# Row means removed inside the turning matrix of a GRU stage: a four-layer graph network on one Trainium2 core

## Chip, core and metric

One NeuronCore of a Trainium2 chip runs the whole program. The metric is the device time of one execution in microseconds (us). Three timed runs of the kernel before gave 720.81, 721.02 and 722.56, median 721.02. A further execution was taken with the hardware profiler; it took 719.45, and its span, from the first to the last recorded instruction, is 717.7.

## What is computed

3327 nodes with 64 features each, an adjacency matrix of zeros and ones, and four layers, each of the form x = x + layer(relu(layernorm(x))):

- 0: attention in hyperbolic space (curvature 1), a sum over neighbours weighted by a sigmoid and an arctangent-like distance;
- 1: a decay sum over neighbours, times a weight matrix, plus a bias;
- 2: a signed graph attention with two GRU cells;
- 3: the hyperbolic attention again, with a learned curvature r.

The parts that matter here:

```python
def _layernorm(x, axis=-1, eps=1e-5):
    m = jnp.mean(x, axis=axis, keepdims=True)
    v = jnp.var(x, axis=axis, keepdims=True)
    return (x - m) / jnp.sqrt(v + eps)
...
def gru_cell(x, h, w_ih, w_hh, b_ih, b_hh):
    ...
    return (1.0 - z) * n + z * h
```

A layer's output is multiplied by the diagonal of the adjacency matrix (dcol below) where the masks of the fast path ask for it, and added to x; then the next layer takes the row mean, the row variance, and the relu of what is normed.

## The kernel before, in words

The nodes are padded to 26 tiles of 128 rows. X holds all of x in SBUF as 128 partitions x 26 tiles x 64 features; tiles 0 to 12 and 13 to 25 are the two halves ("HALVES", "(h t)" in X2). One program does the four layers one after the other; each is planned by hand: inside tc.manual_schedule the instructions of an engine run in the order in which they are written, and an instruction that waits holds up those behind it on its engine.

**Layer 2, plain_gat (L1841).** The attention sums run block by block on PE (block, L1865, matmuls L1871), into four PSUM tiles, one for each group of columns in COLS: group 0 has 4 tiles of each half, groups 1, 2 and 3 have 3. A dictionary `todo` (L1944) hangs small work of the other engines behind certain blocks: `inverse` behind block 12 (degree maximum L1934 on DVE, then a relu, logarithm and exponential on ACT), `inverse2` behind block 17 (L1941, L1942 on DVE). Then two GRU cells run over the four groups, eight steps in a software pipeline: gate matmuls (products, L1987 and L1992), sigmoids (L2000) and tanh (L2011) on ACT, state on DVE (L2007 to L2027).

**Turning back.** The GRU output lies with features on the partitions. turn_back(k) (L2032) brings group k back to rows: for every tile of the group PE multiplies up to four terms, one after the other into the same PSUM place, by the identity (L2043; group 3 has a single term and uses a transpose, L2041). Group k takes PSUM bank 4 + k; two neighbouring banks make one "slot", and waits are kept by slot, so that groups 0 and 1 share one and groups 2 and 3 another. scale(k) multiplies by the diagonal, on ACT tile by tile with the diagonal's column as the scale (L2059), for group 3 on DVE (L2054); use(k) adds the product to X on DVE (L2063). The end of plain_gat:

```python
tanh(K - 1)
scale(0)
turn_back(1)
scale(1)
turn_back(2)
state(K - 1)
use(0)
turn_back(3)
use(1)
scale(2)
...
```

**Layer 3, hyperbolic_series (L350).** It opens with the layer norm: the row mean by halves (L449, L450), X minus mean into H (L452), squares on ACT (L453), relu and its square on ACT (L455, L456), the row sums of both squares (L458, L466, L469), and between them the inverse root by bit tricks (root_by_bits, L125: eight dependent DVE steps on 128x26 values). L472 multiplies the norms' squares by the inverse variance. From there a chain of 26-wide DVE steps leads to Xr, the normed and scaled features (L481), their fp16 parts hi and lo (L482, L484), the transposes on PE (L542, L517), the attention vectors (L560 to L578) and the main loop (L877). POOL meanwhile builds extra columns from x2 (L493 to L506) and, before that, zeroes X0 (L436) and sets constants in Xe (L437, L439). The "late" tiles of the adjacency matrix, loaded by SP (L1447), are only counted for zeros (L1459) during the main loop.

The main loop runs four column chunks by 26 blocks: sigmoid (ACT, L629), mask (POOL, L632), distance matmuls (PE, L643, L644), arctangent (ACT, L649), weights (DVE, L654), sums (PE, L664, L672). After it come the sums' way back and about seventy 26-wide steps (factors, L721) that end in the factors ah and am (L858, L860).

**The tail (L912 to L930).** X becomes X + ah Xr + am M. DVE does Xr (L916, L919). ACT multiplies the first 22 tiles of M by am, one instruction a tile with am's column as its scale (L923); DVE does the last four ("own") and adds M in three pieces, each stored at once by SP (L2104).

hyperbolic_series serves layer 0 too, where x arrives by DMA.

Of the kernel before, what the change touches and what calls it, by code (L numbers as in the profile page):

```python
# [49 lines left out]
def tile_gnn4(ctx: ExitStack, tc: tile.TileContext, x, adjT, att0, b0, w1, bias1, w_gat, a_gat,  # L50
# [296 lines left out]
            after.append(of_r)  # L347
        return wlr, bcol, cc, sqc, isqc, um2, maxn2

    def hyperbolic_series(r, params, ok, masks=None, done=None, ahead=None, then=None, checks=None):  # L350

# [10 lines left out]


        KE = D + 9
        left_row = rows[0 if r is None else 1]
        W = 512
        with ExitStack() as st:
# [60 lines left out]
            with room(name="hsp", bufs=1) as tp, room(name="hsps", bufs=2, space=PSUM) as ps, \  # L430
                    tc.manual_schedule(engines={mybir.EngineType.Activation, mybir.EngineType.DVE,
                                                mybir.EngineType.PE, mybir.EngineType.Pool}):
                H, R, sq, sr = [tp.tile([P, T, D], F32, name=n) for n in ("H", "R", "sq", "sr")]
                Xe = tp.tile([P, T, KE + 9], F16, name="Xe")
                E, Fe = Xe[:, :, D:KE], Xe[:, :, KE:]
                G.memset(X0, 0.0)  # L436
                G.memset(E[:, :, 6:], SX)  # L437
                for k, part in enumerate(f16_parts((1.0 - PB / PA) * SX)):
                    G.memset(Fe[:, :, 6 + k:7 + k], part)  # L439
# [4 lines left out]
                    return tp.tile([P, T], F32, name=name)  # L444


                mean, v, rv, ax, ia2 = [new(n) for n in ("mean", "v", "rv", "ax", "ia2")]
                for ts in HALVES:
                    V.reduce_sum(mean[:, ts], X[:, ts, :], axis=AX.X)  # L449
                V.tensor_scalar(mean, mean, 1.0 / D, None, op0=OP.mult)  # L450
                for ts in HALVES:
                    V.tensor_sub(H[:, ts, :], X[:, ts, :], wide(mean[:, ts]))  # L452
                    A.activation(sq[:, ts, :], H[:, ts, :], AF.Square)  # L453
                for ts in HALVES:
                    A.activation(R[:, ts, :], H[:, ts, :], AF.Relu)  # L455
                    A.activation(sr[:, ts, :], R[:, ts, :], AF.Square)  # L456
                for ts in HALVES:
                    V.reduce_sum(v[:, ts], sq[:, ts, :], axis=AX.X)  # L458
                V.tensor_scalar(v, v, 1.0 / D, LN_EPS, op0=OP.mult, op1=OP.add)
                sd, q1, q2 = new("sd"), new("q1"), new("q2")  # L460
                steps = root_by_bits(sd, q1, q2, v)
                next(steps)
                V.reciprocal(rv, v)
                for _ in range(3):
                    next(steps)
                V.reduce_sum(x2[:, HALVES[0]], sr[:, HALVES[0], :], axis=AX.X)  # L466
                for _ in steps:
                    pass
                V.reduce_sum(x2[:, HALVES[1]], sr[:, HALVES[1], :], axis=AX.X)  # L469
                if r is not None:  # L470
                    V.tensor_scalar(rv, rv, cc, None, op0=OP.mult)
                V.tensor_mul(x2, x2, rv)  # L472
                V.tensor_scalar(ax, x2, 1.0, None, op0=OP.subtract)
                V.reciprocal(ia, ax)
                V.tensor_scalar(root, x2, 1.0, None, op0=OP.max)
# [90 lines left out]
                    copy_on(on, XF[c][:, o, :], turned16(lambda t: Xp[:, t, D:], KE, *range(t, t + c[1])))  # L566
                V.tensor_mul(right, lr[:, :, 1], z)
                V.tensor_scalar(right, right, bcol, None, op0=OP.add)
                V.scalar_tensor_tensor(root, root, ROOT, zs, op0=OP.mult, op1=OP.mult)
                V.tensor_scalar(small["k"], ia, 0.5 * PF, None, op0=OP.mult)  # L570
                V.tensor_scalar(small["bx"], ax, -1.0, None, op0=OP.mult)
# [340 lines left out]
            with room(name="hse", bufs=1) as tp:  # L912
                ah, am = all_factors(tp)

                def scaled(a, f, ts):
                    V.tensor_mul(a[:, ts, :], a[:, ts, :], wide(f[:, ts]))  # L916

                def added(a, ts):
                    V.tensor_add(X[:, ts, :], X[:, ts, :], a[:, ts, :])  # L919

                own = slice(T - 4, T)
                for t in range(own.start):
                    A.activation(M[:, t, :], M[:, t, :], AF.Copy, scale=am[:, t:t + 1])  # L923
                for ts in HALVES:
                    scaled(Xr, ah, ts)
                    added(Xr, ts)
                scaled(M, am, own)
                for ts in HALVES[0], slice(T // 2, T - 6), slice(T - 6, T):
                    added(M, ts)
                    done(ts)  # L930
# [907 lines left out]

            then(H, hparts, banks, last_x, finish, close)

    def plain_gat(masks, zo, deg, first, wg, gru, H, parts, banks, last_x, finish, close):  # L1841

# [6 lines left out]
        with ExitStack() as st:  # L1851
# [47 lines left out]
            xh = [[pers.tile([P, HP], F32, name=f"xh{g}{o}") for o in range(2)] for g in range(2)]  # L1899
            oP = H.rearrange("p k o d -> p (k o d)")  # L1900
            wgT = pers.tile([D, D], F32, name="wgT")
            hundred = pers.tile([P, 1], F32, name="hundred")
            V.memset(hundred, -100.0)
            for _ in range(1):
# [35 lines left out]
                def inverse2():  # L1940
                    V.scalar_tensor_tensor(deg, deg, -1.0, r0, op0=OP.mult, op1=OP.mult)  # L1941
                    V.scalar_tensor_tensor(deg, deg, 2.0, r0, op0=OP.add, op1=OP.mult)  # L1942

                todo = {3: lambda: degrees(2, 4), 4: lambda: degrees(3, 6), 12: lambda: (weights2(4), inverse()),  # L1944
                        13: lambda: turn(0, 6), 15: lambda: weights3(5), 17: inverse2, 19: lambda: turn(4, 7),
                        20: lambda: turn(8, 4), 23: lambda: turn(12, 6)}
                V.tensor_scalar(zo[:, 2 * T:2 * T + 2], zo[:, 2 * T:2 * T + 2], first, None, op0=OP.mult)
# [84 lines left out]
                def turn_back(k):  # L2032

                    terms = [oP] if k == C - 1 else [oP, hP, deg] if k > 1 else [oP, xh[0][0], hP, deg]
                    t0, n = COLS[k]
                    pt = turned[k] = bank(4 + k)
                    for t in range(n):
                        cs = slice((t0 + t) * P, (t0 + t + 1) * P)
                        for i, src in enumerate(terms):
                            if len(terms) == 1:  # L2040
                                PE.transpose(pt[:, t * P:(t + 1) * P], src[:, cs], ident)  # L2041
                            else:
                                PE.matmul(pt[:, t * P:(t + 1) * P], src[:, cs], ident, start=i == 0,  # L2043
                                          stop=i == len(terms) - 1)

                def of_bank(k):
                    n = COLS[k][1]
                    return turned[k][:, :n * P].rearrange("p (t h d) -> p h t d", h=2, d=D)

                def scale(k):  # L2050
                    t0, n = COLS[k]
                    o = scaled[k] = tp.tile([P, 2, 4, D], F32, name="x", bufs=2)
                    if k == C - 1:
                        V.tensor_mul(o[:, :, :n, :], of_bank(k),  # L2054
                                     d2[:, :, t0:t0 + n, None].to_broadcast([P, 2, n, D]))
                        return
                    for h in range(2):
                        for t in range(n):
                            A.activation(o[:, h, t, :], of_bank(k)[:, h, t, :], AF.Copy, scale=d2[:, h, t0 + t:t0 + t + 1])  # L2059

                def use(k):
                    t0, n = COLS[k]
                    V.tensor_add(X2[:, :, t0:t0 + n, :], X2[:, :, t0:t0 + n, :], scaled[k][:, :, :n, :])  # L2063

                for k in (2, 3):
                    mean(k)
# [18 lines left out]
                tanh(K - 1)  # L2085
                scale(0)
                turn_back(1)
                scale(1)
                turn_back(2)
                state(K - 1)  # L2090
                use(0)
                turn_back(3)
                use(1)
                scale(2)
                scale(3)
                use(2)
                use(3)

    def load():
        for ts in HALVES:  # L2100
# [10 lines left out]
    wt, bias, wg, gru = middle_weights()  # L2111
    zo = const.tile([P, 2 * T + 2 + EARLY + len(LATE)], F32, name="zo")
    first = const.tile([P, 1], F32, name="first")
    V.memset(first, 0.0)
    for o in (0, D):
        V.memset(first[o:o + 1, :], 1.0)
    with ExitStack() as ms:
        mid, rs = [ms.enter_context(ExitStack()) for _ in range(2)]
        masks = [None] * (T // 2)
        degs = []  # L2120

        def make_masks(ks):
            pool = ms.enter_context(room(name=f"masks{ks[0]}", bufs=1, side="right"))
            for k in ks:
                masks[k] = pool.tile([P, 2, NP], F8, name=f"mask{k}")

        def right():
            make_masks(range(T // 2 - EARLY // 2))
            pool = rs.enter_context(room(name="middle", bufs=1, side="right"))
            degs.append(pool.tile([P, NP // 2], F32, name="deg"))  # L2130
            return degs[0]

        make_masks(range(T // 2 - EARLY // 2, T // 2))
        pool = mid.enter_context(room(name="own", bufs=1))
        own = [pool.tile([P, 2, CW], F32, name=f"own{k}") for k in range(2)]
        hyperbolic_series(None, params, ok[:, 0:1], ahead=Ahead(masks, zo, own),
                          then=lambda e: plain_decay(
                              e, right, masks, zo, wt, bias, gru, of_r[0],
                              lambda *a: plain_gat(masks, zo, degs[0], first, wg, gru, *a)))
        rs.close()  # L2140
        mid.close()
        hyperbolic_series(r3, params3, ok[:, 2:3], masks, store, checks=Late(zo))
    V.reduce_sum(ok[:, 1:2], zo, axis=AX.X)


# [55 lines left out]
```

## Time and profile before

| | us |
|---|---|
| median of three runs | 721.02 |
| the profiled execution's own time | 719.45 |
| its span | 717.7 |
| PE busy | 636.2 (89%) |
| DVE busy | 532.8 (74%) |
| ACT busy | 542.1 (76%) |
| POOL busy | 433.4 (60%) |

Times in the texts below are read from the start of the span. The stages: layer 0 until about 245, layer 1 until about 388, the blocks of layer 2 until 427, its GRU steps until 447.4, turning back and adding until 461.3, layer 3's norm and preparation until 486, its main loop until 694, the tail until 717.7.

PE is busy in nearly all of this, apart from the first microseconds, the stretch between turning back (last matmul at 458.4) and the first transposes of layer 3 (474.7), and the tail. Where PE is idle, DVE and ACT set the time.

In the views, an instruction's "start" and length are those of the profiler; a matmul of fp32 operands counts as two instructions; back-to-back instructions of one engine may overlap by some hundredths of a microsecond; "idle before" names what released an engine after a wait. "PEclk" is the granted clock of PE as a share of full speed.

### The profile page before, as it was taken

How to read it: one execution, taken by the hardware profiler on the slowest of the kernel's cores; microseconds unless marked ns; L12 is line 12 of the kernel's file. 1: busy time of each engine (PE TensorE's matmuls, PEld its weight loads, DVE VectorE, ACT ScalarE, POOL GpSimd, SP SyncE). 2: the span in 40 equal slices, each digit the busy share in tenths (PEclk: the TensorE clock that was granted, in tenths of full speed). 3: DMA queues.
4: the chain of work that ended last, by engine and by line, in shares of the span. 5: the costliest groups of instructions: out<-in, count | busy, mean ns of one | idle time of the engine just before them, and what ended most of it. 6: DMA issues, size and time to landing. Idle time of an engine off the chain costs nothing.

```text
span 717.7 us, 12120 instructions
## 1 busy us (share of the span) xinstructions
PE 636.2 (89%) x4291; PEld 261.4 (36%) x4291; DVE 532.8 (74%) x990; ACT 542.1 (76%) x718; POOL 433.4 (60%) x329
## 2 busy tenths in 40 slices
PE   0799999999999889989998999459999999999970
PEld 0522233333333333435445653443223433333320
DVE  5967778777777799999755428697776877778756
ACT  3688888888888695687881479359888888888853
POOL 2799999989999400205730000039888788887840
PEclk9999999999999999999999999969999999999995
DMA  3998888898878716489960000203325345443001
GB/s 64 313 301 274 259 268 266 277 288 273 268 245 271 258 69 215 137 291 333 402 243 1 2 1 1 95 18 96 89 82 147 105 120 146 116 119 115 25 1 52
DMA packets 61638, 119.25 MB, mean 166 GB/s; under 512 B 9568, under 2 KB 34048, under 8 KB 61568
## 3 DMA queue, kind: packets, MB, share of 16 engines
q1 hardware_dynamic: 57216, 118.38, 51.2%
q10 hardware_dynamic: 4352, 0.02, 0.3%
q8 instruction: 35, 0.57, 0.3%
q14 instruction: 35, 0.29, 0.1%
HBM read 115.64 MB, written 0.88 MB: 162 GB/s over the span
## 4 chain that ended last, share of the span: by engine, by line
PE 67%; DVE 12%; issue 6%; POOL 6%; ACT 4%; DMA 3%; ACTq 1%; POOLq 0%; DVEq 0%
PE slot L664 17%; PE slot L672 9%; PE slot L643 9%; PE slot L1564 9%; PE slot L644 8%; POOL sig L632 6%; PE slot L1578 5%; PE slot L1871 5%; DMA adj<-in 3%; PE slot L1987 2%; PE slot L2043 1%; PE slot L1992 1%; DVE X L1617 1%; ACTq L322 1%; ACT sig L629 1%
## 5 line engine op out<-in xcount | busy, mean ns | idle before, releaser
L654 DVE SCALAR_TENSOR_TENSOR sig<-slot,sig 128x768 f32<-128x768 f32 (+2 forms) x209 | 212.8, 1018 | 105.6 <-POOL sig L632 104.2
L649 ACT ACTIVATE slot<-slot 128x768 f32<-128x768 f32 (+1 forms) x208 | 177.2, 852 | 53.3 <-PE slot L644 53.1
L632 POOL TENSOR_TENSOR sig<-adj,sig 128x768 f32<-128x768 f32 (+2 forms) x105 | 201.7, 1943 | 12.9 <-ACT sig L629 8.4
L629 ACT ACTIVATE sig<-leftB,right 128x768 f32<-128x768 f32 (+2 forms) x210 | 203.5, 970 | 0.5 <-PE pt L517 0.5
L632 POOL TENSOR_TENSOR sig<-mask,sig 128x768 f32<-128x768 fp8e4 (+3 forms) x106 | 173.6, 1651 | 38.2 <-ACT sig L629 37.3
L664 PE MATMUL slot<-sig,Xr 128*64 128x384 f32 (+1 forms) x832 | 169.9, 526 | 3.7 <-DVE sig L654 3.4
L643 PE MATMUL slot<-XC,XT 128*128 128x384 f16 (+1 forms) x416 | 142.2, 342 | 3.1 <-ACT sum L682 1.7
L644 PE MATMUL slot<-XF,XE 73*128 73x384 f16 (+1 forms) x416 | 141.6, 340 | 0.0
L672 PE MATMUL slot<-sig,X 128*32 128x384 f32 (+1 forms) x832 | 94.2, 525 | 0.0
L1570 ACT ACTIVATE w<-slot,ebias 128x832 bf16<-128x832 f32 x76 | 69.0, 951 | 25.3 <-PE slot L1564 24.9
L664 PEld LDWEIGHTS slot<-sig,Xr 128*64 128x64 f32 x832 | 49.8, 135 | 85.7 <-issue 62.7
L643 PEld LDWEIGHTS <-XT 128*128 128x128 f16 x416 | 40.6, 98 | 93.8 <-issue 67.4
L1564 PE MATMUL slot<-mask,rest 128*128 128x416 fp8e4 x208 | 53.9, 341 | 5.0 <-ACT adj L1570 2.8
L1564 PE MATMUL slot<-mask,after 128*128 128x416 fp8e4 x208 | 53.4, 339 | 1.3 <-DVE deg L1588 1.3
L644 PEld LDWEIGHTS <-XE 73*128 73x128 f16 x416 | 40.8, 98 | 28.6 <-issue 4.0
L1459 DVE TENSOR_SCALAR_CACHE_REDUCE same<-late 128x832 fp8e4<-128x832 f32 x48 | 48.4, 1009 | 0.0
L219 POOL TENSOR_TENSOR mask<-mask,offdiag 128x128 fp8e4<-128x128 fp8e4 x26 | 17.5, 684 | 44.4 <-PE slot L1564 44.3
L436 POOL MEMSET X<- 128x832 f32 x2 | 1.6, 791 | 69.6 <-ACT xh L1978 69.6
L1871 PE MATMUL slot<-mask,own 128*64 128x384 fp8e4 (+1 forms) x416 | 39.6, 345 | 2.6 <-DVE deg L1588 2.6
L672 PEld LDWEIGHTS slot<-sig,X 128*32 128x32 f32 x832 | 16.4, 108 | 67.7 <-issue 67.7
L542 PE MATMUL pt<-ident_h,Xp 128*64 128x128 f16 x32 | 2.6, 314 | 37.7 <-ACT Xp L482 37.7
L1578 PE MATMUL slot<-w,h 128*64 128x416 bf16 x304 | 34.0, 345 | 0.0
(341 smaller groups left out, 696.2 us busy)
## 6 DMA issues: line engine op xcount, KB each, us to landing
adj<-in SPq DMA_DIRECT2D x78, 384.0 KB, 5.2
late<-in SPq DMA_DIRECT2D x48, 416.0 KB, 3.2
adj<-in SPq DMA_DIRECT2D x17, 832.0 KB, 7.2
adj<-in SPq DMA_DIRECT2D x27, 512.0 KB, 5.8
ahead<-in SPq DMA_DIRECT2D x14, 832.0 KB, 7.7
ahead<-in SPq DMA_DIRECT2D x16, 416.0 KB, 5.7
own<-in SPq DMA_DIRECT2D x16, 416.0 KB, 5.8
own<-in SPq DMA_DIRECT2D x8, 832.0 KB, 10.1
```

Source lines behind the costliest of these rows:

```text
L629: A.activation(sig[:, os], leftB[c][:, os], AF.Sigmoid, bias=right[:, b:b + 1])
L632: G.tensor_tensor(sig[:, os], adj[:, os], sig[:, os], op=OP.mult)
L643: PE.matmul(L[:, o, :c[1] * P], XT[:, rows], XC[c][:, o, :], start=True, stop=False)
L644: PE.matmul(L[:, o, :c[1] * P], XE[:KE, rows], XF[c][:, o, :], start=False, stop=True)
L649: A.activation(L, L, AF.Arctan, scale=PA / SX ** 2)
L654: V.scalar_tensor_tensor(sig[:, os], slot[:, os, :tiles[k][0][1] * P], PC, sig[:, os], op0=OP.add, op1=OP.mult)
L664: PE.matmul(acc[c][o * D:(o + 1) * D, 0, :n], Xr[:, b, :], sigs[k][:, o, :], start=b == 0, stop=b == T - 1)
L672: PE.matmul(acc[c][q:q + 32, 1, :n], X0[:, b - 1 + i, :], w[:, o, :], start=b == 1, stop=b == T - 1, tile_position=(0, q))
L1564: PE.matmul(cnt[o][:, h, :BK], w, cols(k, o, h), start=w is after and steps[k][1] == T - 1, stop=True, skip_group_check=True)
L1570: A.activation(ws[k][:, o, :, :], cnt[o][:, :, :BK], AF.Exp, scale=-LN2, bias=ebias)
L1578: PE.matmul(acc[c][o * D:(o + 1) * D, h, :BK], parts[i][:, b, :], w[:, o, h, :], start=b == T - 1 and i == 0, stop=b == 0 and i == 1)
L1871: PE.matmul(acc[k][o * D:(o + 1) * D, :], w, mask[:, of(k, o * HP)], start=n == 0 and i == 0, stop=n == T - 1 and i == 1)
```

## The change

The row mean of layer 3's norm is taken off in two places, both ahead of layer 3, and put back at the end:

- **centre**, behind block 12 of layer 2, takes the row means of the X that layer 2 started from and subtracts them from X; the means are kept in ln.mean.
- **centring**, a 128x130 matrix, stands in for the identity in turn_back. Its 128 columns are the identity minus 1/64 in each half's block, so that what comes out is already free of its row mean; two more columns give the means themselves, which new_means multiplies by the diagonal and adds to ln.mean. Every term goes through a matmul; groups have PSUM banks (4, 6, 0, 2) and up, so each lies in a slot of its own.
- X after layer 2 is then X minus its row mean. The squares, positives, squares of the positives and their row sums are formed group by group as the groups are added (squares, positive, squares_of_positive on ACT; variance, norms2 on DVE). Group 1 is scaled and added by DVE straight from PSUM in six products (use_at_once). The inverse root moves to the end of plain_gat.
- hyperbolic_series, when given ln, skips its mean, H, squares and sums, and uses X, ln.rv, ln.sd and ln.x2. X0 is zeroed on ACT (a copy of X times 0) instead of POOL.
- The mean comes back to the last four tiles of X by four ACT additions in the preparation, and to the other 22 in the tail: L923 becomes an Identity with am as scale and ln.mean as bias.

Layer 0 takes the old path (ln is None). The diff, cut to its core:

```diff
+        own = slice(T - 4, T)
...
-                G.memset(X0, 0.0)
+                if ln is None:
+                    G.memset(X0, 0.0)
+                else:
+                    A.activation(X0.rearrange("p t e -> p (t e)"), X[:, HALVES[0], :].rearrange("p t d -> p (t d)"),
+                                 AF.Copy, scale=0.0)
...
+                else:
+                    H, rv, sd = X, ln.rv, ln.sd
...
-                V.tensor_mul(x2, x2, rv)
+                V.tensor_mul(x2, x2s, rv)
...
                 V.tensor_scalar(right, right, bcol, None, op0=OP.add)
+                if ln is not None:
+                    for t in range(own.start, own.stop):
+                        A.activation(X[:, t, :], X[:, t, :], AF.Identity, bias=ln.mean[:, t:t + 1])
...
                 for t in range(own.start):
-                    A.activation(M[:, t, :], M[:, t, :], AF.Copy, scale=am[:, t:t + 1])
+                    A.activation(M[:, t, :], M[:, t, :], AF.Identity, scale=am[:, t:t + 1], bias=ln.mean[:, t:t + 1])
...
+            BACK = P + 2
+            centring = pers.tile([P, BACK], F32, name="centring")
+            means = centring[:, P:]
+            G.memset(means, 0.0)
+            for o in range(2):
+                G.memset(means[o * D:(o + 1) * D, o:o + 1], 1.0 / D)
+            V.tensor_sub(centring[:, :P].rearrange("p (o d) -> p o d", o=2), ident.rearrange("p (o d) -> p o d", o=2),
+                         wide(means))
...
+                def centre():
+
+                    V.reduce_sum(ln.mean, X, axis=AX.X)
+                    V.tensor_scalar(ln.mean, ln.mean, 1.0 / D, None, op0=OP.mult)
+                    V.tensor_sub(X, X, wide(ln.mean))
...
-                    pt = turned[k] = bank(4 + k)
...
+                    for i in range(0, n, 3):
+                        m = min(3, n - i)
+                        pt = bank((4, 6, 0, 2)[k] + i // 3)[:, :m * BACK].rearrange("p (t x) -> p t x", x=BACK)
+                        for t in range(m):
+                            cs = slice((t0 + i + t) * P, (t0 + i + t + 1) * P)
+                            for s, src in enumerate(terms):
+                                PE.matmul(pt[:, t, :], src[:, cs], centring, start=s == 0, stop=s == len(terms) - 1)
...
+                def new_means(k):
+                    t0 = COLS[k][0]
+                    for pt in turned[k]:
+                        ts = slice(t0, t0 + pt.shape[1])
+                        V.tensor_mul(dm[:, :, ts], pt[:, :, P:].rearrange("p t h -> p h t"), d2[:, :, ts])
+                        t0 = ts.stop
...
+                def use_at_once(k):
+                    t0, n = COLS[k]
+                    for h in range(2):
+                        for t in range(n):
+                            to = X2[:, h, t0 + t, :]
+                            V.scalar_tensor_tensor(to, of_bank(k, h, t), d2[:, h, t0 + t:t0 + t + 1], to,
+                                                   op0=OP.mult, op1=OP.add)
...
-                scale(1)
                 turn_back(2)
                 state(K - 1)
+                turn_back(3)
                 use(0)
-                turn_back(3)
-                use(1)
+                squares(0)
+                positive(0)
+                use_at_once(1)
+                new_means(0)
+                new_means(1)
+                squares(1)
+                variance(0)
+                variance(1)
                 scale(2)
                 scale(3)
+                use(3)
+                squares(3)
                 use(2)
-                use(3)
+                squares(2)
+                for k in (0, 1, 3, 2):
+                    if k:
+                        positive(k)
+                    squares_of_positive(k)
+                variance(3)
+                variance(2)
+                V.tensor_scalar(ln.v, ln.v, 1.0 / D, LN_EPS, op0=OP.mult, op1=OP.add)
+                steps = root_by_bits(ln.sd, *ln.qs, ln.v)
+                next(steps)
+                V.reciprocal(ln.rv, ln.v)
+                for between in (lambda: new_means(2), lambda: new_means(3),
+                                lambda: V.tensor_add(ln.mean, ln.mean, dm.rearrange("p h t -> p (h t)"))):
+                    next(steps)
+                    between()
+                norms2(0, COLS[2][0])
+                for _ in steps:
+                    pass
+                norms2(COLS[2][0], C2 - COLS[2][0])
```

## Prediction

> **What bounds the kernel now.** I first read the busy shares and the 40 slices of the page: PE is busy nearly everywhere, but for a hole late in the span. The chain of waits over 447 to 473 us shows who ends last there (start, length, engine, tile, line):
>
> ```profile
> 447.49 3.78 PE slot L2043 x32
> ...
> 451.30 1.75 ACT x L2059 x8
> ...
> 453.10 4.96 PE slot L2043 x42
> 458.05 0.34 PE slot L2041 x3
> ...
> 458.42 1.34 ACT x L2059 x6
> ...
> 459.78 0.56 DVE x L2054
> 460.34 0.95 DVE X L2063 x2
> ...
> 461.31 1.96 DVE mean L449 x2
> ...
> 465.49 1.97 DVE v L458 x2
> ...
> 471.37 0.20 DVE x L472
> ```
>
> PE turns the GRU output back in two bursts with ACT's scaling between them; then ACT, then DVE work alone. From the last matmul (458.39) to L472, where the squared norms are first used, 13 us pass. The waits of 447 to 472 us (waiter, releaser: total us, times, longest) show the false step in the middle:
>
> ```profile
> DVE X L2063 <- ACT x L2059: 3.4, 1, 3.4
> PE slot L2043 <- ACT x L2059: 1.8, 1, 1.8
> DVE x L2054 <- ACT x L2059: 1.8, 1, 1.8
> ```
>
> PE's second burst waits for ACT though its own operands are ready at 449.1: the two groups share one PSUM slot. The table by stage shows that PE has nothing to do until L472 has run:
>
> ```profile
> 447.40:458.40 11.00, 9.14 (x81) 8.69 (x77) 6.98 (x14) 4.76 (x17) 0.24 (x4) 1.00 0.00 0
> 458.40:471.40 13.00, 0.00 (x0) 0.00 (x0) 11.21 (x24) 6.49 (x12) 0.31 (x3) 0.68 0.38 131
> ```
>
> Columns: PE, PEld, DVE, ACT, POOL busy, granted clock, DMA. The second place that the change touches is the tail, from the timeline:
>
> ```profile
> 705.36 5.36 ACT L923 ACTIVATE M<-M,am 128x64 f32<-128x64 f32 x22 [5.20 <-DVE am L860]
> ...
> 709.34 2.03 DVE L919 TENSOR_TENSOR X<-X,M 128x832 f32<-128x832 f32 x3
> ...
> 710.44 1.43 SPq L2104 DMA_DIRECT2D out<-X  x3
> ```
>
> ACT ends at 710.72 and DVE's last add starts at 710.8: ACT sets the end, with nothing to spare.
>
> **Part 1, matmuls.** 37 of the 40 tile matmuls keep their operands and stream 130 columns for 128. In the first burst of the old trace 16 matmuls start at 447.42, 447.75 and then every 0.224 us up to 450.88 (timeline of PE); I scale that to 0.227 (bounds: unchanged, if the weight load sets it, or +2%; 0.15 us in all). The three transposes L2041 become matmuls of that pitch. With a slot for each group, the second group waits for operands alone (latest the state of its columns, 449.1), the third for its state at 451.2, the fourth for the last state at 453.42. So PE runs through: 447.75 + 15 x 0.227 = 451.16, + 12 x 0.227 = 453.88, + 9 x 0.227 = 455.92, + 3 x 0.227 = 456.60. A result is there 0.17 us later (the old first burst: 450.88 + 0.224 = 451.10, ended at 451.27). Groups are ready at 451.33, 454.05, 456.09 and 456.77, instead of 451.28, 456.05, 458.05 and 458.39.
>
> **Part 2, the chain to the norms.** Durations: DVE 128x384 0.55, 128x512 0.69, next one 0.08 earlier if independent; reductions 0.55 (384), 0.68 (512), 1.08 (896), 0.94 (768); 26-wide steps 0.2 each when dependent. ACT from SBUF without a pointer by L456 (832 wide: 0.897, next 0.80 later): I take off 0.80 ns an element, the slope between L710's forms of 384 and 512 (490 and 592 ns): 0.54 for 384 and 0.64 for 512. The new 64-wide products from PSUM lie between L1617's pitch from SBUF, 0.197, and its full length, 0.28; I take 0.197, since L2007 from PSUM (0.615 at 384) is no slower than its kind. The means' products go by L705 (0.16, pitch 0.1).
> - ACT scales group 0 until 453.10; DVE ends the state at 453.42, adds group 0 by 454.03, does the six products of group 1 from 454.07 to 455.33, three small products by 455.6, the sums of squares of groups 0 and 1 by 456.7.
> - ACT meanwhile: squares and positives of group 0, 454.06 to 455.25; squares of group 1 wait for DVE until 455.36 and end at 455.9. Behind that wait in ACT's queue stands the scaling of group 2, but its matmuls end at 456.09 anyway: 456.11 to 457.45.
> - DVE: group 3 scaled 456.79 to 457.35, added by 457.93; group 2 added by 458.4; their variance sums wait for ACT's squares (458.5, 459.0) and end at 459.55.
> - ACT: seven positives and their squares, three of them after a wait for the one before: 458.9 to 462.6. This hides beside DVE, with hardly 0.1 us to spare.
> - DVE: variance, root and reciprocal with the small products between: 459.55 to 460.9; first norm sum (896) to 462.0; four root steps; second norm sum 462.66 to 463.6. The product of L472 starts at **463.63 instead of 471.37: 7.7 us earlier**.
>
> The old mean, subtraction, squares and halves (L449 to L469) are gone. What follows L472 keeps its instructions and order, so 471.4 to 486 moves as it stands. The zeroing of X0, formerly on POOL, is an 832-wide ACT copy that waits for the second norm sum (its memory): 463.6 to 464.5, while ACT's next work came 2.4 us after L472: hidden, and 0.9 us if it were not. The four mean additions to the last tiles stand ahead of the leftB copy in ACT's queue, where ACT waits 1.83 us for PE (481.12 to 482.95); by L923 they take 1.05 us. The fourth "late" load now waits for the second norm sum, about 463.6; the XC transfers behind it on SP are due at 471.4, and the first check that reads a late tile starts after 489 in the old trace: no cost.
>
> **Part 3, before.** The reduction, scaling and subtraction of the means, 128x1664 each (two halves of L449 and L452: 1.95 + 0.18 + 1.96 = 4.1 us), stand on DVE between the degree maximum (ends 401.0) and inverse2 (410.76, after 9.74 us of waiting for ACT): hidden. PE's blocks run on until 427. POOL's three memsets and DVE's centring product come at about 399, with POOL idle since 368.
>
> **Part 4, the tail.** The 22 products L923 get a bias column beside the scale column. No row has both. The nearest rows show one pointer against none:
>
> ```profile
> L2000 ACT ACTIVATE gate<-slot,gs 128x384 f32<-128x384 f32 x12 | 6.3, 576 | 1.2 <-PE slot L1987 1.1
> L923 ACT ACTIVATE M<-M,am 128x64 f32<-128x64 f32 x22 | 5.4, 333 | 5.2 <-DVE am L860 5.2
> L682 ACT ACTIVATE sum<-slot 128x384 f32<-128x384 f32 x12 | 5.2, 482 | 6.1 <-PE slot L672 6.1
> ```
>
> A bias pointer cost 576 - 482 = 94 ns. Bounds for a second one: nothing, if both are fetched together, or 94 ns again. I take 94: 22 x 0.094 = 2.07 us on ACT, whose end moves from 710.72 to 712.8; DVE's last add and the last store follow, as they waited for it already: **+2.0 us**. The Trainium skill, page "ScalarE: Activation LUTs", section "What ACT_TABLE_LOAD costs", speaks against this edit: each [128,1] pointer adds about 93 ns. By it the tail loses 22 x 0.093 = 2.05 us, by a joint fetch nothing; its 186 + 0.833 x 64 + 93 = 332 ns agrees with L923's 333 with one pointer, and no row here has two.
>
> **Sum.** -7.7 + 2.0 = -5.7 us on the profiled execution: span 717.7 to 712.0, its time 719.45 (1.75 more than the span) to 713.75. The three timed runs have a median of 721.02, 1.57 above the profiled one, so I predict 721.0 - 5.7 = **715.3**. The clock leaves an uncertainty: granted 1.00 up to 463, 0.50 until 480.0, that is 5.3 us past PE's first matmul at 474.74. PE's pause shrinks from 16.4 to 10.4 us, still far more than the 4.6 us after which the clock fell. Where the rise falls may differ: the 26 transposes L517 took 2.89 us at half clock, so at most about 1.4, +-0.7 us.
>
> **Rivals.**
> - The second pointer is free (for: scale and bias may come in one fetch; against: 94 ns for the first). -7.7 alone: 713.3. Chance 0.20.
> - The new chain overlaps less: the six products 0.28 each (+0.5), ACT's squares and positives without their six overlaps of 0.09 (+0.5), a dozen handoffs between ACT and DVE late by 0.08 each (+1.0): 717.3. For: the two release each other in turn, with 0.1 us of slack. Or the slots do not free PE, and its second burst still starts at 453.1: the same 2.0 us. Against: the changed program's waits there name the state's operations alone. Together 0.20.
> - Little comes out at all: both of these and a worse clock phase, within 0.3%: 0.05.
> - Slower: DVE's centring product stands ahead of the degree maximum and waits for a POOL memset whose memory must be released. Behind it: maximum, ACT's logarithm and exponential, inverse2, all due by 427.24, where L1973 reads them. Slack: 405.86 - 401.02 = 4.8 us ahead of ACT, 427.24 - 414.58 = 12.7 us behind it, so nothing is lost until 416.3; from 422 on the loss exceeds the gain. At worst the memory is held until PE's blocks end at 427: +10.7 - 5.7, 726. For: POOL's memset L437 waited 19.4 us for its memory in this trace. Against: the waits of the changed program name sums of the layer before (L1578), done by 390. Chance 0.03.
>
> **Chances.** Forecast 0.50, the rest as above, 0.02 for below 712.5. The range 712.5 to 718 takes in the free pointer (713.3 - 0.7) and the poorer overlap (717.3 + 0.7). A measurement of this kernel can tell about 0.3% (2.2 us) from no change: faster 0.92, same 0.05, slower 0.03.
>
> **What would show it.** L472's successor starts near 463.6; the turning matmuls run in one burst without a wait on ACT and end near 456.7; the L923 group's mean is near 426 ns instead of 333, and the last add starts 7.7 us after am is done, now 710.8 - 705.14 = 5.7. It would be wrong if ACT's chain of squares ends well after 462.6, if the centring product starts after 416, or if the 22 products stay at 333 ns.

## The result, and the profile after

The changed kernel took 714.15 us (median of four runs, 711.85 to 715.24) beside 721.37 for the kernel before (four runs, 720.81 to 722.56): ratio 0.9894, 95% interval 0.9866 to 0.9921. A second comparison, made with later experiments, gave 716.9 (seven runs) beside 721.8 (twelve): 0.9935, interval 0.9908 to 0.9963. Predicted was 715.3, a gain of 5.7 us; the two comparisons gave 7.2 and 4.9.

The profiled execution took 714.2, its span is 712.4, against 717.7 before. I cut both spans at the same events and compare the lengths:

| stretch | before | after | difference |
|---|---|---|---|
| start to the first turning matmul | 447.42 | 446.43 | -0.99 |
| to the product of norms and inverse variance (L472, now L483) | 23.95 | 16.01 | -7.94 |
| to the first weights on DVE (L654, now L668) | 15.82 | 18.06 | +2.24 |
| to the factor am (L860, now L874) | 217.95 | 218.15 | +0.20 |
| to the end of the last addition (L919, now L933) | 6.23 | 8.21 | +1.98 |
| to the end of the span | 6.33 | 5.54 | -0.79 |
| sum | 717.7 | 712.4 | -5.30 |

The first row is no effect of the change: over the twelve traces of this study it lies between 446.3 and 450.3, and the kernel as changed shows 446.43 in one trace and 450.27 in another. This scatter of 4 us is also in every time of a whole run given below, so the experiments are read by their stretches. The other rows can be compared to some hundredths, but for one cause that is found below.

**Turning back.** Timeline of PE in the kernel after (start, length, engine, line, operation, tiles, shape):

```profile
446.98 0.39 PE L2069 MATMUL slot<-centring,hP 128*128 128x130 f32 x2
...
454.13 0.39 PE L2069 MATMUL slot<-centring,own 128*128 128x130 f32 x2
454.35 0.39 PE L2069 MATMUL slot<-centring,hP 128*128 128x130 f32 x2
```

PE runs through without a wait on ACT; the pitch is (454.35 - 446.98) / 33 = 0.223, as with 128 columns. DVE and ACT behind it, from their timelines:

```profile
452.99 1.24 DVE L2108 SCALAR_TENSOR_TENSOR X<-slot,dcol,X 128x64 f32<-128x64 f32 x6
...
457.41 1.02 DVE L2130 TENSOR_REDUCE wt<-xh 128x6 f32<-128x384 f32 x2
...
461.46 0.94 DVE L2133 TENSOR_REDUCE wt<-xh 128x12 f32<-128x768 f32 x1
462.44 0.19 DVE L483 TENSOR_TENSOR x<-wt 128x26 f32<-128x26 f32 x1
```

```profile
460.74 0.52 ACT L2126 ACTIVATE xh<-xh 128x384 f32<-128x384 f32 x1
462.44 0.90 ACT L442 ACTIVATE X<-X 128x832 f32<-128x832 f32 x1 [1.18 <-DVE wt L2133]
```

The six products of group 1 take 1.24 together, one every 0.194 (forecast 1.26 and 0.197). ACT ends its squares at 461.26, just before DVE's last row sum starts at 461.46: as forecast, ACT is hidden by a hair. The zeroing of X0 (L442) comes right behind and delays nothing. The product of L483 stands at 462.44, 16.01 after the first turning matmul; the forecast was 463.63 - 447.42 = 16.21.

**The preparation of layer 3** is where the forecast did not see something. ACT's timeline after, up to its first sigmoids:

```profile
472.26 1.05 ACT L582 ACTIVATE X<-X,mean 128x64 f32<-128x64 f32 x4
475.39 0.60 ACT L535 ACTIVATE leftB<-pe 128x512 f32<-128x512 f32 x1 [2.08 <-PE pe L590]
477.11 2.38 ACT L643 ACTIVATE sig<-leftB,right 128x512 f32<-128x512 f32 x3 [1.12 <-DVE XE L533]
```

and the same place before:

```profile
482.95 0.60 ACT L524 ACTIVATE leftB<-pe 128x512 f32<-128x512 f32 x1 [1.83 <-PE pe L576]
483.45 1.32 ACT L629 ACTIVATE sig<-leftB,right 128x512 f32<-128x512 f32 x2
```

Before, the first sigmoid started as soon as leftB was copied. Now it waits another 1.12 us for the copies of Xe's transposes (L533). It reads nothing of Xe. But H, R, sq and sr are no longer allocated, so the tiles of layer 3 lie elsewhere, and by the order of allocation the program's first sigmoid tile now lies where Xe was: it may be written only after Xe's last transpose, which ends on PE at 477.02, just before the sigmoid starts. The four mean additions (L582) are hidden, since ACT waits 2.08 us for PE behind them.

**The tail**, from the groups of lines with shapes kept apart, and the timeline:

```profile
L936 ACT ACTIVATE M<-M,mean,am 128x64 f32<-128x64 f32 x22 | 7.4, 426 | 5.2 <-DVE am L874 5.2
```

```profile
698.87 7.40 ACT L936 ACTIVATE M<-M,mean,am 128x64 f32<-128x64 f32 x22 [5.20 <-DVE am L874]
...
703.32 1.02 DVE L933 TENSOR_TENSOR X<-X,M 128x832 f32<-128x832 f32 x1 [0.38 <-ACT M L936]
705.64 1.22 DVE L933 TENSOR_TENSOR X<-X,M 128x448 f32<-128x448 f32 x2 [1.30 <-ACT M L936]
```

The mean of the products went from 333 to 426 ns, and DVE's additions wait for them twice (0.38 and 1.30).

### The profile page after: what moved, and what is told of

Same layout as the page of the kernel before. It is cut to its first block, busy times and chain, and to the rows that moved or that the text cites. A ratio compares the mean times of both kernels' runs of the same rounds, so it can differ in the third digit from the quotient of the medians.

```text
span 712.4 us, 12148 instructions
## 1 busy us (share of the span) xinstructions
PE 637.5 (89%) x4294; PEld 263.2 (37%) x4294; DVE 534.8 (75%) x1002; ACT 545.5 (77%) x723; POOL 431.6 (61%) x331
## 5 line engine op out<-in xcount | busy, mean ns | idle before, releaser
L668 DVE SCALAR_TENSOR_TENSOR sig<-slot,sig 128x768 f32<-128x768 f32 (+2 forms) x209 | 212.6, 1018 | 106.2 <-POOL sig L646 103.6
L1622 POOL TENSOR_TENSOR X<-X,bias 128x256 f32<-128x256 f32 (+1 forms) x7 | 5.3, 788 | 44.5 <-DVE Xr L1637 44.5
```

Of the source, the lines that this page charges most:

```text
L668: V.scalar_tensor_tensor(sig[:, os], slot[:, os, :tiles[k][0][1] * P], PC, sig[:, os], op0=OP.add, op1=OP.mult)
```

## Experiments

What stood open: whether the second pointer is what lengthened the tail; why the preparation grew; which part of the change brought the 7.94; whether the best of it can be had together. "T1" below is from the first turning matmul to the product L483 (L472 before), "T2" from there to the first weights on DVE, "T4" from am to the end of the last addition.

**One pointer in the tail**

```diff
-                    A.activation(M[:, t, :], M[:, t, :], AF.Identity, scale=am[:, t:t + 1], bias=ln.mean[:, t:t + 1])
+                    A.activation(M[:, t, :], M[:, t, :], AF.Identity, scale=am[:, t:t + 1])
```

> The 22 products of M in the tail keep Identity and the scale column, but get no bias column: the row mean is left out of 22 tiles of the output. Theory (the second pointer costs 94 ns an instruction): they take 333 ns each again, and from the end of am to the end of DVE's last add it is 6.2 us as before the change, not 8.2. Rival (Identity is slower than Copy, whatever its operands): 426 ns each, 8.2 us.

This kernel leaves the row mean out of 22 tiles of the output. Measured: 713.27 in one run; T4 is 6.22, as before the change. The group of its products:

```profile
L936 ACT ACTIVATE M<-M,am 128x64 f32<-128x64 f32 x22 | 5.4, 334 | 5.2 <-DVE am L874 5.2
```

With Identity kept and the bias gone, the mean is 334 ns again. So it is the second pointer that costs 92 ns, about the 94 that the rows of before gave for a first one, and not the change from Copy to Identity. Yet the span loses less than the 1.99 us: from am to the end of the span the changed kernel takes 13.75 and this one 12.28, that is 1.5. Behind the last addition the seven traces with two pointers take 5.5 to 5.8 us, the five without 6.0 to 6.4. With waits between the additions the three stores are issued over 2.85 us instead of 1.42; that the earlier stores are then out of the last one's way fits, and was not tried by itself.

**Xe elsewhere**

```diff
+                if ln is not None:
+                    pads = [tp.tile([P, T, D], F32, name=f"pad{i}") for i in range(4)]
                 Xe = tp.tile([P, T, KE + 9], F16, name="Xe")
```

> Four unused tiles of the size of H, R, sq, sr stand ahead of Xe again, so that Xe lies where it lay before the change. From the first product with the norms' squares to the first product of the weights in the main loop it was 15.8 us before the change and 18.1 after it. Theory (the first sigmoid waits for the last transpose of Xe because its tile took over Xe's memory): the sigmoid starts right behind the leftB copy, and the stretch is about 17.0. Rival (all of the 2.2 us come from the PE clock, which rose later): the stretch stays near 18 while the clock rises as late.

Measured: 712.87; T2 is 15.75 instead of 18.06. ACT's timeline:

```profile
475.17 0.60 ACT L537 ACTIVATE leftB<-pe 128x512 f32<-128x512 f32 x1 [0.88 <-PE pe L592]
475.66 1.32 ACT L645 ACTIVATE sig<-leftB,right 128x512 f32<-128x512 f32 x2
```

The wait for the copies of Xe's transposes (L533) is gone, and the growth with it. The unused tiles move everything allocated behind them, so the run shows that the place in memory matters; that it is Xe's place is read from the name of the wait and the order of allocation. But the clock of PE also rose earlier in this trace than in that of the changed kernel, so that one run could not say how much belongs to the memory.

**Idle matmuls, first try**

```diff
                 turn_back(3)
+                for _ in range(42):
+                    PE.matmul(bank(7)[:, :P], ident, ident, start=True, stop=True)
                 use(0)
```

> 42 idle matmuls (the identity by itself, into an unused PSUM bank) follow the turning matmuls, so that PE works through its pause. Theory (half clock in the preparation costs about 1 us of the 2.2, the rest is the memory wait): the granted clock stays at 1.00 from 456 us on, the eight matmuls of leftB take 1.2 us and not 2.0, and the stretch from the norms to the first weights is 15.5 to 17.0. Rival (the memory wait alone): 18 as after the change, with PE's steps shorter and nobody the earlier for it. A second rival: the idle matmuls slow DVE and ACT, and the stretch from the first turning matmul to the norms, 16.0 after the change, grows.

Measured: 726.79, T1 27.8. It missed its aim, though T2 came out at 16.80, with leftB at full clock. Its waits (waiter, releaser: total, times, longest):

```profile
ACT xh L2119 <- DVE X L2108: 12.1, 1, 12.1
DVE X L2108 <- PE slot L2163: 12.0, 1, 12.0
```

Bank 7 is in the slot of group 1. DVE's products of group 1 (L2108) come after the idle matmuls in program order, so they waited for all of them, though they read another bank, long done. A slot's reader waits for every matmul written into the slot ahead of it.

**Groups 1 and 2 in one slot again**

```diff
-                        pt = bank((4, 6, 0, 2)[k] + i // 3)[:, :m * BACK].rearrange("p (t x) -> p t x", x=BACK)
+                        pt = bank((4, 6, 7, 2)[k] + i // 3)[:, :m * BACK].rearrange("p (t x) -> p t x", x=BACK)
```

> Groups 1 and 2 of the turning matmuls share a PSUM slot (banks 6 and 7), as pairs of groups did before the change. Theory (a slot of its own frees PE): group 2 waits until DVE has read group 1, about 1.6 us more, and the stretch from the first turning matmul to the first product with the norms grows from 16.0 to about 17.6. Rival (the chain of squares on ACT and DVE sets that stretch, PE has time): 16.0 to 16.3.

Measured: 718.4; T1 17.75, 1.74 more. The size is as expected, the mechanism is not: PE's burst was not interrupted. Again the reader paid:

```profile
DVE X L2108 <- PE slot L2069: 2.0, 1, 2.0
```

DVE's products of group 1 waited for the matmuls of group 2, which were queued behind group 1 and ahead of the products in program order.

**The changed kernel again**

> The changed kernel as it is, beside the kernel before, for the interval and as the measure for the runs sent with it. All theories: 712 to 715, 6 to 8 us under the kernel before; from the factors am to the end of the last addition 8.2 us; from the product L483 to the first weights 17 to 18 us, depending on where the clock of PE rises.

Measured: 716.9, 4.9 under the kernel before; 712 to 715 and a gain of 6 to 8 were expected. In its trace the first turning matmul alone starts 3.84 us later than in the first trace. T1 16.00, T4 8.21, and T2 16.97, 1.1 less than in the first trace of the very same kernel. The tables by stretch show what differs: the granted clock (columns: PE, PEld, DVE, ACT, POOL busy, clock, DMA share, GB/s). First trace of the changed kernel, then this one:

```profile
457.80:474.88 17.08, 8.79 (x90) 8.22 (x91) 15.23 (x55) 10.61 (x22) 6.91 (x16) 0.50 0.28 85
474.88:480.50 5.62, 5.49 (x46) 3.37 (x46) 3.08 (x14) 3.99 (x6) 2.58 (x3) 1.00 0.03 8
```

```profile
464.26:474.50 10.24, 4.62 (x62) 4.18 (x62) 9.61 (x30) 6.20 (x11) 6.97 (x16) 0.50 0.15 44
474.50:483.24 8.74, 8.22 (x75) 5.70 (x73) 5.93 (x25) 5.84 (x13) 2.58 (x3) 1.00 0.16 39
```

In the first, the half clock lasted 17.08 us, to 12.4 us after L483; in this one 10.24, to 8.2 after it. Between those two moments PE turns leftB, which the first sigmoid needs. PE's lines for it, first trace and this one:

```profile
471.95 2.02 PE L590 MATMUL junk<-ident,left 128*128 128x128 f32 x8
473.76 1.59 PE L590 MATMUL pe<-ident,left 128*128 128x128 f32 x8
```

```profile
475.70 1.16 PE L590 MATMUL junk<-ident,left 128*128 128x128 f32 x8 [0.15 <-DVE left L574]
476.70 1.06 PE L590 MATMUL pe<-ident,left 128*128 128x128 f32 x8
```

**The mean added in the main loop, and Xe elsewhere**

```diff
-                    A.activation(M[:, t, :], M[:, t, :], AF.Identity, scale=am[:, t:t + 1], bias=ln.mean[:, t:t + 1])
+                    A.activation(M[:, t, :], M[:, t, :], AF.Copy, scale=am[:, t:t + 1])
...
+                if ln is not None and 48 <= j <= 50:
+                    ts = slice(9 * (j - 48), min(9 * (j - 47), T))
+                    V.tensor_add(X[:, ts, :], X[:, ts, :], wide(ln.mean[:, ts]))
...
-                if ln is not None:
-                    for t in range(own.start, own.stop):
-                        A.activation(X[:, t, :], X[:, t, :], AF.Identity, bias=ln.mean[:, t:t + 1])
```

(and the four unused tiles of the second experiment)

> The mean is added back to all 26 tiles by three DVE additions inside the main loop (behind blocks 48, 49 and 50) instead of four ACT additions and a bias in 22 products; four unused tiles put Xe at another place, so that the first sigmoid's tile no longer shares its memory. Theory that the second pointer cost 2.0 us at the end and the shared memory 1.05 in the preparation: from am to the last addition 6.2 instead of 8.2, from the product L483 to the first weights 15.7 to 17.0 instead of 18.1, the main loop longer by no more than 0.6 (DVE waits for ACT's sigmoids there): 3.0 to 4.0 us under the changed kernel of the same call, 710 to 711. Rival: DVE is what bounds the main loop at that point, and the three additions of some 0.7 us each lengthen it by 2.1: then about 1.5 us under it.

Measured: 713.63 (six runs, 711.28 to 717.55), 3.3 under the changed kernel measured beside it, as expected, though not the 710 to 711 named; against the kernel before 0.9894, interval 0.9861 to 0.9927. T4 is 6.22, the wait for Xe is gone, T2 is 16.92, and the main loop takes 218.15, as in the changed kernel. With Xe elsewhere alone it took 217.97, so that 3.7 us of additions on DVE (1250 ns for 576 columns) cost at most 0.2 us there. Since T2 had the late clock here, the trace again mixes two causes; the table below separates them.

**The same with idle matmuls, and idle matmuls alone**

```diff
                 norms2(COLS[2][0], C2 - COLS[2][0])
+                for _ in range(42):
+                    PE.matmul(bank(7)[:, :P], ident, ident, start=True, stop=True)
```

> As the run before it, and besides 42 idle matmuls on PE behind the turning, up to about 466, behind which nothing waits but PE's own next transposes. Theory that the late rise of the clock costs some 1.2 us after the product L483: granted clock full from 447 to 470 at least, the 26 transposes of hi take 1.5 us instead of 2.9 and leftB's matmuls 1.1 instead of 2.0, and from the product to the first weights 14.3 to 15.5: 0.5 to 1.5 us under the run before it. Rival: PE's speed is hidden there beside DVE and ACT, or the clock falls all the same; then no difference.

> The changed kernel with the 42 idle matmuls behind the turning alone. It replaces the run in which they delayed DVE: here every reader of the PSUM slot is written before them. Theory that the shared memory (1.05) and the late clock (1.26) are two costs: from the product L483 to the first weights 18.06 - 1.26 = 16.8, or down to 15.6 where the faster transposes count as well; the first sigmoid still waits for Xe. Rival: the growth of the preparation comes from the shared memory alone, and the clock is chance: 18.0.

Measured: 712.5 with the other two edits (six runs, 711.27 to 713.37; 0.9870, interval 0.9842 to 0.9897), 717.79 alone (one run). T2 is 16.63 and 18.08. The idle matmuls kept the clock full over the transposes of hi, and then it fell after all. So the 14.3 to 15.5 and the 15.6 to 16.8 of the two theories were missed, and the 18.0 of the second rival came out without a test of it, since leftB again had the half clock. Idle matmuls alone, by stretch:

```profile
466.03:475.68 9.65, 6.96 (x102) 6.03 (x102) 9.11 (x28) 6.98 (x14) 6.92 (x16) 1.00 0.21 57
475.68:479.10 3.42, 3.42 (x21) 3.40 (x21) 2.11 (x12) 0.45 (x2) 0.00 (x0) 0.50 0.25 58
479.10:484.11 5.01, 4.88 (x39) 2.77 (x38) 2.47 (x9) 3.69 (x6) 2.58 (x3) 1.00 0.02 5
```

A short stretch of 3.42 us at half clock fell just on leftB. So the faster transposes of hi (2.0 us of PE instead of 2.96) gained nearly nothing, and what counts is the clock under leftB, as the table below bears out. The 1.1 us between the medians of the last kernel and the one without idle matmuls are within the spread of their runs and not settled.

**Slots alone, on the kernel before**

```diff
-                    pt = turned[k] = bank(4 + k)
+                    pt = turned[k] = bank((4, 6, 0, 2)[k])
```

> The kernel before, its four turned groups in PSUM banks 4, 6, 0 and 2 instead of 4, 5, 6 and 7, so that each has a slot of its own; nothing else. From the first turning matmul to the product L472, 23.95 us in the kernel before. Theory that the shared slots held PE's second burst for ACT: one burst of some 9 us without a wait on ACT, and the product 1.7 to 2.3 us earlier: 21.7 to 22.2. Rival: ACT, which scales 20 tiles at 0.223, ends no earlier, and the slots bring less than 0.5: 23.5 or more.

Measured: 716.48 beside 722.81; T1 21.06, a gain of 2.89, more than expected. One burst without a wait accounts for 2.0 of it. The rest is the trap of the slot's reader once more, which I had overlooked in the trace of before:

```profile
458.42 1.33 ACT L2059 ACTIVATE x<-slot,dcol 128x64 f32<-128x64 f32 x6 [1.00 <-PE slot L2041]
459.78 0.56 DVE L2054 TENSOR_TENSOR x<-slot,dcol 128x384 f32<-128x384 f32 x1 [1.78 <-ACT x L2059]
```

ACT's scaling of group 2 waited for the transposes of group 3 (L2041) in the same slot, and DVE's scaling of group 3 for ACT's reading of group 2. With slots of their own, both start when their own matmuls are done; the same two in this run:

```profile
455.81 1.34 ACT L2059 ACTIVATE x<-slot,dcol 128x64 f32<-128x64 f32 x6 [0.67 <-PE slot L2043]
456.14 0.56 DVE L2054 TENSOR_TENSOR x<-slot,dcol 128x384 f32<-128x384 f32 x1 [0.41 <-PE slot L2041]
```

**No groups**

In the changed kernel, squares, positives and row sums over whole halves behind the last addition:

```diff
+                use(3)
+                use(2)
...
+                for h in range(2):
+                    A.activation(half(sq, h), of_x(h), AF.Square)
+                for h in range(2):
+                    A.activation(half(pos, h), of_x(h), AF.Relu)
+                    A.activation(half(sr, h), half(pos, h), AF.Square)
+                for h in range(2):
+                    V.reduce_sum(halves(ln.v)[:, h, :], sq.rearrange("p (h t d) -> p h t d", h=2, d=D)[:, h], axis=AX.X)
```

> The changed kernel with the squares, positives and row sums formed over the two halves after the last addition, as the kernel before did, and no longer group by group; mean removal and slots stay. From the first turning matmul to the product L483, 16.0 us with groups. Theory that the groups hide a part of ACT's squares beside the additions: six ACT instructions of 832 columns (0.9, then 0.8 each) begin only after the last addition, the product follows some 6.9 us after it instead of 5.2: 17.2 to 18.2. Rival: the work behind the last addition is what counts in both, the groups bring nothing: 16.0 to 16.4.

Measured: 717.24 in one run; T1 17.79, as the first theory has it: DVE now waits 0.96 for the first squares, and the last positives end later. The groups bring 1.78.

**What T1 is made of.** 23.95 before, 21.06 with slots of their own (-2.89), 17.79 with the means taken off ahead and group 1 added straight from PSUM as well (-3.27, which no run takes apart), 16.01 with the work by groups (-1.78).

**What T2 is made of.** All twelve traces, by where the first sigmoid's tile lies and by the clock under leftB:

| T2 in us | leftB at full clock | leftB at half clock |
|---|---|---|
| first sigmoid's tile not on Xe | 15.82 (before), 15.75 (Xe elsewhere), 15.81 (slots alone) | 16.92 (mean in the loop), 16.63 (with idle matmuls) |
| on Xe | 16.80 (first idle matmuls), 16.97 (changed kernel again), 16.96 (no groups) | 18.06 (changed kernel), 17.94 (one pointer), 18.43 (one slot), 18.08 (idle matmuls alone) |

The two causes add up: 1.1 us for the memory, 0.8 to 1.5 for the clock. The memory belongs to the change and is in every run of it. The clock is not a property of the kernel: the same kernel stands in both columns. Layer 0, whose code the change leaves alone, shows the clock by itself: in three traces (changed kernel again, mean in the loop with idle matmuls, no groups) leftB's first eight matmuls there run at half clock, 2.02 us instead of 1.16, and ACT copies leftB at 30.2 to 30.8 instead of 29.0 to 29.1. That is a part of the scatter of the first stretch; the rest was not looked into.

The main loop adds a little: 218.14 to 218.17 in the seven traces with the tile on Xe, 217.95 to 217.97 in the three of the upper left cell. These 0.2 us go with the memory; why was not tried.

## Why the prediction was right, and where not

- **Part 1, turning matmuls:** right. The pitch stayed at 0.223, the lower bound, instead of 0.227; the burst took 9.20 us from first start to last end (forecast 9.35). The free slots worked, and for a better reason than the one named: not only PE, but the slots' readers were held.
- **Part 2, the chain to L472:** right, 7.94 for 7.7. The six products came every 0.194 (0.197 was put in). ACT's chain of squares was hidden with 0.2 us to spare (hardly 0.1 was worked out). "The chain overlaps less" falls, and so does PE still waiting.
- **"What follows L472 keeps its instructions and order, so 471.4 to 486 moves as it stands":** this is the step that failed. Instructions and order did stay; the addresses did not. Removing four large tiles moved the first sigmoid's tile onto Xe, and a wait appeared that no line of the diff shows: +1.1 us, with the clock up to +2.24. The waits in the changed program, which name what stands ahead of the first sigmoid, tell this beforehand.
- **The clock, given as at most 1.4, +-0.7:** the right worry at the wrong place. It costs 0.8 to 1.5 us, and it sits in leftB's matmuls, not in the transposes of hi. In all twelve traces the stretches of half clock in this part last 3.4, 10.2, 13.7 or 17.1 us, and where the clock was down when PE resumed (ten traces), the rise came 3.3 to 9.8 us after its first transposes. 17.08 / 5, 13.65 / 4 and 10.24 / 3 are all 3.41 to 3.42: falls and rises lie on a raster of 3.41 us, and where it lies against the program differs from run to run. The Trainium skill, page "TensorE: Matmul & The Clock Gate", section on the HAM clock gate (Part 1), says that the gate watches free-running windows of 3413 ns which do not start with the kernel. The traces agree to some nanoseconds. The same section has the clock rise after at least one busy window. Not every step that the profile shows as busy was enough here: in the first trace of the changed kernel PE was busy for 3.38 of the 3.41 us from 468.05 to 471.46, with fp16 transposes and small matmuls, and the clock rose only a step later.
- **Part 3, centre and centring:** hidden, as forecast: DVE's centring product stands at 397.81, far ahead of the 416 from which it would have cost, the three steps of centre end at 404.16, and DVE then still waits 5.61 us for ACT. The rival "slower" falls.
- **Part 4, the tail:** right, and the rival of a free second pointer falls: 426 ns, T4 +1.98 for +2.0. The Trainium skill's 93 ns for each pointer ("ScalarE: Activation LUTs", "What ACT_TABLE_LOAD costs") agrees with 426 - 333 = 93. What I did not see is that some 0.5 us comes back behind the last addition.
- **The sum** of -5.7 met -5.3 in the traces, but with errors on both sides: the preparation 2.24 too good in it, the end of the tail 0.8 and the luck of the first stretch 1.0 too bad. That the median came within 1.2 us of 715.3 is in part luck too: the second comparison of the same kernels gave a gain 2.3 us smaller.

## What to carry to other kernels

When an edit removes large tiles, read the new waits of everything that is allocated after them, since a stage whose code is unchanged may now lie on another tile's memory; here it took back 1.1 us of 7.9. Where waits are kept by a larger unit than the data (a slot of two banks), look at the readers too: they wait for whatever was issued into the unit ahead of them, so that the order of issue, not only of need, sets the time. Work that costs a pointer in a tail where ACT sets the end can be nearly free as plain DVE work in a main loop with slack: the version with the mean added there and Xe kept apart ran at 713.6, and with idle matmuls besides at 712.5, beside 716.9 for the changed kernel.

## Hardware behaviour that I had not expected

- fp32 matmuls of 130 columns ran at the pitch of 128 (0.223 us).
- A second [128,1] pointer on a 64-wide ACT product cost 92 to 93 ns, about as much as a first one (94, from rows of another width).
- The granted clock moves on a raster of 3.41 us with a phase of its own: the same program shows 10.2 or 17.1 us of half clock at the same place. Over a stretch with PE mostly idle, a difference of 1 us between two single traces can be this alone. Counted back in steps of 3.41 us from the fall, the step in which the turning ended was the one that closed with the fall where PE had been busy for 31 to 37% of it (four traces); where it was 43 to 66% (five traces), the clock fell a step later. The share alone is no rule: behind the idle matmuls the clock fell at the end of steps with 66 and 73% (two traces), in which fp16 transposes and small matmuls ran.
- A DVE addition of 576 columns took 1250 ns in the main loop, beside 1015 for 832 columns in the tail of the same trace. The broadcast operand is not what slows it: centre's subtraction (L1971 in that run), with the same operands and POOL and ACT idle, took 1894 ns for 1664 columns, 1.14 ns a column beside 2.17. What else in the loop does it was not tried.
